# Diffusion one row tile ahead of the attention's products instead of three

## The chip, the cores and the metric

The kernel runs on one core of one Trainium2 chip. The metric is the device time of one execution in microseconds (us). A core has five engines that run beside each other: TensorE (PE in the profile, with its weight loads as PEld) multiplies matrices into PSUM, VectorE (DVE), ScalarE (ACT) and GpSimd (POOL) compute on tiles in SBUF and PSUM, and SyncE (SP) issues the DMA transfers. Each engine takes its instructions from a queue of its own, in order; where one engine needs the result of another, it waits on a semaphore.

## The reference

Four graph layers are applied to 3327 nodes with 256 features, each followed by a residual addition and a normalization over the features. The first three (neighbour mean, graph convolution with a Mamba block, graph attention) are not changed. Layer 3 is what matters here:

- `R = adj + I`, each row divided by its sum. Two steps are taken, n = 0 and 1, from `Xf = Xa = X`.
- In each step a top-p attention matrix `A` is made from `Xa`: `logits = q @ k.T`, a softmax over each row, then only the largest probabilities whose sum before them is below 0.9 are kept, and the row is divided by what is kept.
- The diffusion is `Xf = R @ Xf`, the attention `Xa = A @ Xa`, and `Z = Z + Xf @ U1[n].T + Xa @ U2[n].T`.
- The result is a layernorm of `X + Z` with gain and bias, then the residual and the last normalization.

## The kernel before

All arrays are float32. The nodes are padded to 26 row tiles of 128. A row tile of either matrix product, `R @ Xf` or `A @ Xa`, is a sum over 26 column tiles, that is 26 products of 128x128 by 128x256 on TensorE. The profile counts two matmul records for each such product.

Layer 3 runs as two passes over the row tiles, one for each step: pass 0 (the loop at L1163) and pass 1 (L1194). For a row tile a pass needs:

- the *scores* (`scores`, L803): q times k into PSUM (L817), copied by ACT into the row's `e` tile (L823 in pass 0; the copy made in program order, recorded as L801, in pass 1). One PSUM tile (`sc`, one buffer) is used for all of them.
- the *search* for the row's threshold. In pass 0 it is `search_short` (L916): maxima on DVE, one exponential over the row on ACT (L924), the thresholded row on DVE (L927). In pass 1 it is `search_long` (L933): two exponentials (L948, L950) and four counting passes (L963, L965, L995, L997) on ACT, and on DVE selections (L1015, L882, L1045) and at last the thresholded row (L1053). It is spread over three iterations of the loop by `yield`.
- the *diffusion* (`diffused`, L843, and `aggregated`, L829): GpSimd makes the row's own term `t` (L847, and in pass 1 with `s` loaded at L850 and added at L851), TensorE makes 26 products (L837) with adjacency blocks that SP loads in six transfers (L835, ring `at` of three buffers), and DVE writes the result `xf` (L856).
- the *attention's products* (`attended`, L859): groups of four 128x128 transposes of `e` (L866), copies out of PSUM on ACT (L868, or L801 in pass 1), and products (L870).
- the end of the row: in pass 0 `first` (L1063), which transposes `xf` and the attention's result (L1071) and multiplies them by the U matrices (L1078 to L1085); in pass 1 `second` (L1094), which reads `xf` at L1097, normalizes and stores.

How far the diffusion runs ahead is set by `DL`. In iteration i the rows to be diffused are

```
more = range(len(xfs), min(nt, i + DL + 1))
```

(L1167 and L1204), and `xf` has a ring of `DL + 2` buffers (L855). In pass 0 the first of these rows is emitted together with the scores of row i + 1 and any further ones after them; then follow the attention's products of row i. In pass 1, `slot` (L1207) deals out the diffusion's products between the steps of the scores, of the attention of row i - 1 and of the searches:

```
for _ in range(products * len(more)):
    next(spread, None)
```

The text of the program gives an order of work; the framework's scheduler then places the instructions on each engine's queue within the dependencies. Instructions passed through `here` or `in_order` keep the order of the text among themselves (in pass 1 the score products and copies, and ACT's six sweeps of the search); in pass 0 the score products have priority instead. Diffusion products have neither and are placed where the scheduler finds room for them.

With DL = 3, pass 0 diffuses rows 0, 1 and 2 in its first iteration (i = -1), then row i + 3 in iteration i, and nothing in the last three. Pass 1 begins at i = -2 with rows 0 and 1, then row 2 (i = -1), then row i + 3, and nothing from i = 23 on.

Of the kernel before, what the change touches and what calls it, by code (L numbers as in the profile page):

```python
# [35 lines left out]
UNDER = 24.0  # L36
HUGE = 1e38
J3 = 5
DL = 3
KC = 416  # L40


# [1 line left out]
def gnn_kernel(ctx: ExitStack, tc: tile.TileContext, n: int, a: dict, out: bass.AP):  # L44
# [546 lines left out]
    with tc.tile_pool(name="l3", bufs=1) as pool, tc.tile_pool(name="l3d", bufs=1, space=DRAM) as dram:  # L591
# [251 lines left out]
        def diffused(work, atp, psum, p, it, out, each=J3):  # L843

            rd = rdeg[:, it:it + 1]
            t = work.tile([P, D], F32, name="t")
            nc.gpsimd.tensor_scalar(t, (Y if p else X)[:, it, :], rd, None, op0=ALU.mult)  # L847
            if p:
                s = work.tile([P, D], F32, name="s")
                nc.sync.dma_start(s, sd[it])  # L850
                nc.gpsimd.tensor_tensor(t, t, s, op=ALU.add)  # L851
            for acc in aggregated(atp, psum, it, Y if p else X, each):
                if acc is None:
                    yield
            d = work.tile([P, D], F32, name="xf", bufs=DL + 2)  # L855
            nc.vector.scalar_tensor_tensor(d, acc, rd, t, op0=ALU.mult, op1=ALU.add)  # L856
            out.append(d)
# [291 lines left out]
        with tc.tile_pool(name="l3w", bufs=2) as work, tc.tile_pool(name="l3s", bufs=4) as sm, \  # L1149
# [3 lines left out]
            def start(p, t, es, searches, search):  # L1153
                q = work.tile([2 * DA, P], F32, name="q")
                nc.sync.dma_start(q, qd[p][t])
                es[t] = work.tile([P, npad], F32, name="e", bufs=4)
                searches[t] = search(work, sm, es[t], *(x[p][:, t:t + 1] for x in (tots, vs, kepts)),
                                     **({"halves": True} if p and t == nt - 1 else {}))
                return scores(work, psum, p, q, es[t])

            with tc.tile_pool(name="l3p", bufs=2, space=PSUM) as psum:
                es, searches, xfs, todo = {}, {}, [], None
                for i in range(-1, nt):  # L1163
                    parts = []
                    if i + 1 < nt:
                        parts.append(start(0, i + 1, es, searches, search_short))
                    more = range(len(xfs), min(nt, i + DL + 1))  # L1167
                    for j in more[:1]:
# [22 lines left out]
            with tc.tile_pool(name="l3q", bufs=3, space=PSUM) as psum:  # L1191
                es, searches, xfs = {}, {}, []
                result = iter(())
                for i in range(-2, nt + 1):  # L1194
# [7 lines left out]
                    if i + 2 < nt:  # L1202
                        logits = start(1, i + 2, es, searches, search_long)
                    more = range(len(xfs), min(nt, i + DL + 1))  # L1204
                    spread = (x for j in more for x in diffused(work, atp, psum, 1, j, xfs, 1))
# [188 lines left out]
```

## Time and profile before

| | |
|---|---|
| three timed runs, median | 3727.61 us |
| lowest and highest | 3721.43 and 3730.53 us |
| span of the profiled execution | 3731.3 us |
| busy PE, PEld | 3418.9 us (92%), 2538.2 us (68%) |
| busy DVE, ACT, POOL | 2581.8 us (69%), 1699.4 us (46%), 560.9 us (15%) |
| layer 3, pass 0: from its first score product to the last product of `first` | 1935.4 to 2851.8 us |
| layer 3, pass 1: from the first diffusion product to the end | 2852.5 to 3731.3 us |
| diffusion products, pass 0 and pass 1 | 307.9 and 348.0 us busy, 1352 records each |

How to read the profile: times count from the start of the span. A busy time is summed over instructions, so that overlapping ones count twice. A wait is the idle time of an engine ahead of an instruction, and it is put down to the instruction that released it. In a timeline each line is one instruction, or several alike in a row (xcount): start, duration, engine, line, operation, tile written <- tiles read, and in brackets the idle time before it and what ended it. The share of busy time is an average over the whole span; layer 3's two passes have different limits, so each is read by itself, in windows.

### The profile page before, as it was taken

The numbers are of one execution on the slowest core, as the hardware profiler recorded it, in microseconds if no ns is written. First come the engines' busy times: TensorE is split into PE (matmuls) and PEld (weight loads), VectorE is DVE, ScalarE is ACT, GpSimd is POOL, SyncE is SP. The second block draws the span as 40 slices with busy tenths as digits, with TensorE's granted clock in tenths as the row PEclk, the third lists the DMA queues.
The fourth block names the chain that finished last, engine by engine and source line by source line (L and its number), as shares of the span: only waits on it lengthen the run. The fifth ranks groups of instructions, "written<-read, shape, count | busy, mean of one in ns | idle before, by whom it ended". The sixth has DMA issues, their size and how long they took to land. (4 is left out here: it accounts for less than half of the span.)

```text
span 3731.3 us, 41342 instructions
## 1 busy us (share of the span) xinstructions
PE 3418.9 (92%) x14823; PEld 2538.2 (68%) x14823; DVE 2581.8 (69%) x5213; ACT 1699.4 (46%) x2716; POOL 560.9 (15%) x850
## 2 busy tenths in 40 slices
PE   9999998889888877699989999999999999999985
PEld 7888876555454433378867787787777677777764
DVE  1111588999999999877754444445451899999996
ACT  1000655644445564211122333333333888888883
POOL 0000012320211100011110000000000233333332
PEclk9999999989999888899989999999999999999998
DMA  7443343333333121144422221121112222222210
GB/s 243 138 139 98 104 110 97 94 82 94 88 89 88 51 56 47 39 154 145 145 92 86 61 61 53 57 64 51 56 46 62 78 57 65 66 66 66 65 39 7
DMA packets 151985, 307.87 MB, mean 83 GB/s; under 512 B 19858, under 2 KB 73266, under 8 KB 151634
## 3 DMA queue, kind: packets, MB, share of 16 engines
q1 hardware_dynamic: 151762, 305.06, 27.5%
q8 instruction: 120, 1.97, 0.2%
q14 instruction: 103, 0.84, 0.1%
HBM read 294.36 MB, written 10.65 MB: 82 GB/s over the span
## 5 line engine op out<-in xcount | busy, mean ns | idle before, releaser
L553 PE MATMUL y<-db,ident 128*128 128x512 f32 (+3 forms) x1024 | 439.9, 572 | 63.1 <-DVE db L547 63.1
L478 DVE TENSOR_TENSOR_SCAN db<-dA,db 128x2052 f32<-128x2052 f32 (+3 forms) x128 | 463.7, 3623 | 0.9
L553 PEld LDWEIGHTS y<-db,ident 128*128 128x128 f32 x1024 | 200.0, 210 | 255.5 <-issue 157.5
L870 PE MATMUL acc<-G,wt 128*128 128x256 f32 x1352 | 338.3, 394 | 18.3 <-ACT wt L801 17.8
L870 PE MATMUL acc<-X,wt 128*128 128x256 f32 x1352 | 343.6, 391 | 9.0 <-ACT wt L868 8.6
L837 PE MATMUL acc<-F,at 128*128 128x256 f32 x1352 | 348.0, 385 | 1.1 <-ACT q L611 0.6
L266 PE MATMUL cb<-F,at 128*128 128x256 f32 x1352 | 314.1, 386 | 2.0 <-ACT hn L287 2.0
L116 PE MATMUL acc<-xa,at 128*128 128x257 f32 x1352 | 308.3, 381 | 5.7 <-DMA at<-in_adjT 5.7
L870 PEld LDWEIGHTS acc<-X,wt 128*128 128x128 f32 x1352 | 242.5, 189 | 103.9 <-issue 41.3
L837 PE MATMUL acc<-X,at 128*128 128x256 f32 x1352 | 307.9, 381 | 0.6 <-DMA at<-in_adjT 0.6
L746 PE MATMUL acc<-F,at 128*128 128x257 f32 x1352 | 303.8, 381 | 0.8 <-ACT r L719 0.8
L870 PEld LDWEIGHTS acc<-G,wt 128*128 128x128 f32 x1352 | 250.9, 193 | 78.6 <-ACT wt L801 48.5
L266 PEld LDWEIGHTS cb<-F,at 128*128 128x128 f32 x1352 | 260.4, 194 | 60.9 <-issue 16.3
L882 DVE MAX8 cand<-e 128x8 f32<-128x128 f32 x676 | 142.2, 278 | 228.3 <-ACT e L823 216.8
L463 ACT ACTIVATE dA<-dt,A_log 128x512 f32<-128x512 f32 (+3 forms) x512 | 292.1, 633 | 4.1 <-DVE dt L420 3.9
L837 PEld LDWEIGHTS acc<-F,at 128*128 128x128 f32 x1352 | 238.5, 190 | 73.9 <-issue 46.6
L116 PEld LDWEIGHTS acc<-xa,at 128*128 128x128 f32 x1352 | 255.1, 190 | 42.9 <-issue 6.4
L837 PEld LDWEIGHTS acc<-X,at 128*128 128x128 f32 x1352 | 253.0, 191 | 41.1 <-issue 8.5
L746 PEld LDWEIGHTS acc<-F,at 128*128 128x128 f32 x1352 | 253.5, 190 | 36.5 <-issue 1.0
L470 DVE TENSOR_TENSOR db<-du,row 128x2052 f32<-128x2052 f32 (+3 forms) x128 | 240.9, 1882 | 47.7 <-PE y L553 37.9
L547 DVE TENSOR_TENSOR db<-db,row 128x2048 f32<-128x2048 f32 (+3 forms) x128 | 241.2, 1885 | 26.6 <-ACT carry L481 26.6
L868 ACT COPY wt<-tp 128x512 f32<-128x512 f32 (+1 forms) x182 | 93.5, 557 | 307.8 <-PE tp L866 307.6
(302 smaller groups left out, 5207.3 us busy)
## 6 DMA issues: line engine op xcount, KB each, us to landing
at<-in_adjT SPq DMA_DIRECT2D x102, 832.0 KB, 4.5
at<-in_adjT SPq DMA_DIRECT2D x260, 320.0 KB, 3.0
row<-bc SPq DMA_DIRECT2D x80, 512.0 KB, 4.8
at<-in_adjT SPq DMA_DIRECT2D x52, 576.0 KB, 4.5
at<-in_adjT SPq DMA_DIRECT2D x26, 512.0 KB, 3.6
row<-bc SPq DMA_DIRECT2D x16, 384.0 KB, 4.9
row<-bc SPq DMA_DIRECT2D x16, 256.0 KB, 5.3
xt<-in_xT SPq DMA_DIRECT2D x26, 128.0 KB, 4.1
```

The costliest lines, as they stand in the source:

```text
L116: nc.tensor.matmul(acc, at[:, j, :], rhs[:, j0 + j, :], start=(j0 + j == 0), stop=(j0 + j == nt - 1))
L266: nc.tensor.matmul(acc, at[:, j % JC, :], X0[:, j, :], start=(j == 0), stop=(j == nt - 1))
L463: nc.scalar.activation(dA[:, g, 1:], dt[:, g, :], AF.Exp, scale=A[:, g, s:s + 1])
L470: tc.keep_in_program_order(nc.vector.tensor_mul(by_group(dbs[(x[0] * DS + s) % 3], w), du, B[:, 0:1, :].to_broadcast([P, NG, 1 + w])))
L478: nc.vector.tensor_tensor_scan(h[:, :m], dAs[s % 2][:, :m], h[:, :m], initial=0.0, op0=ALU.mult, op1=ALU.add)
L547: nc.vector.tensor_mul(h, h, rows.pop(0)[:, 1:2, 1:].to_broadcast([P, NG, w]))
L553: nc.tensor.matmul(ys[g][:, :w], ident, h[:, g, :], start=False, stop=(s == DS - 1))
L746: nc.tensor.matmul(acc, at[:, j, :], F[:, j0 + j, :], start=(j0 + j == 0), stop=(j0 + j == nt - 1))
L837: nc.tensor.matmul(acc, at[:, j, :], rhs[:, j0 + j, :], start=(j0 + j == 0), stop=(j0 + j == nt - 1))
L868: copy(wt[:, :m, :], pt[:, :m, :])
L870: nc.tensor.matmul(acc, wt[:, j, :], rhs[:, j0 + j, :], start=(j0 + j == 0), stop=(j0 + j == nt - 1))
L882: nc.vector.max(cand[:, s * 8:(s + 1) * 8], z[:, s * SEG:(s + 1) * SEG])
```

## The change

One constant changes. Nothing else in the text does; the two expressions for `more` and the ring of `xf` follow from it.

```diff
@@ -36,7 +36,7 @@
 UNDER = 24.0
 HUGE = 1e38
 J3 = 5
-DL = 3
+DL = 1
 KC = 416
```

With DL = 1, pass 0 diffuses row 0 in iteration -1 and row i + 1 in iteration i, with nothing left for i = 25. Pass 1 diffuses nothing at i = -2, row 0 at i = -1, then row i + 1, and nothing at i = 25 and 26. Each pass still diffuses all 26 rows. The ring of `xf` has three buffers instead of five.

## The prediction

> **What bounds the kernel now.** The change touches layer 3 only, so I looked for where its two passes lie and what each waits for. First the table by stretches and the waits, then the timeline at the three places where the change moves work: the start of pass 0 (1929 us), the hand-over to pass 1 (2852 us), the end.
>
> Waits of pass 0 in its steady part (2040 to 2720 us): waiting engine and line, releaser, us in total, times, longest.
>
> ```profile
> ACT wt L868 <- PE tp L866: 234.9, 79, 9.3
> DVE cand L882 <- ACT e L823: 164.5, 59, 6.3
> ...
> DVE xf L856 <- PE acc L837: 71.5, 20, 3.6
> ...
> PE acc L870 <- ACT wt L868: 4.8, 20, 0.2
> ```
>
> ACT and DVE wait for TensorE; TensorE waits 4.8 us in 680. TensorE bounds pass 0. The row period, from one start of a row's transposes at L1071 to the next (2024.57, 2059.27), is 34.7 us.
>
> Pass 1, steady part: its stretch (busy us of PE, PEld, DVE, ACT, POOL, then clock, DMA), and the only waits of TensorE and of DVE there.
>
> ```profile
> 3111.00:3576.00 465.00, 456.83 (x2197) 338.96 (x2195) 445.32 (x1489) 390.10 (x379) 167.28 (x331) 1.00 0.22 66
> ```
>
> ```profile
> PE tp L866 <- DVE e L1053: 8.2, 15, 0.6
> ```
>
> ```profile
> DVE cs L902 <- DVE top L893: 0.5, 1, 0.5
> ```
>
> Here the bound is DVE: it waits once in 15 rows, while TensorE waits 0.55 us in each row for DVE's last step of a search (L1053). The period is 465/15 = 31.0 us. TensorE has only about half a microsecond to spare per row.
>
> Now the start of pass 1, ACT and TensorE (start us, duration, work, in brackets the idle time before it and what ended it):
>
> ```profile
> 2865.77 3.07 ACT L948 ACTIVATE junk<-e,neg 128x3328 bf16<-128x3328 f32 x1
> ...
> 2881.30 0.85 ACT L801 COPY e<-sc 128x832 f32<-128x832 f32 x1 [12.36 <-PE sc L817]
> 2882.05 3.07 ACT L950 ACTIVATE e<-e,neg 128x3328 f32<-128x3328 f32 x1
> ```
>
> ```profile
> 2868.84 11.52 PE L837 MATMUL acc<-F,at 128*128 128x256 f32 x52 [0.46 <-DMA at<-in_adjT]
> 2880.28 0.97 PE L817 MATMUL sc<-kT,q 64*128 64x416 f32 x4
> ...
> 2932.39 1.97 PE L866 MATMUL tp<-ident,e 128*128 128x128 f32 x8 [6.45 <-DVE e L1053]
> ```
>
> The 52 records are one row's diffusion (26 products, two records each). It stands ahead of the scores of row 1; ACT's copy of those scores stands ahead of the second exponential of row 0 (L950), which has its input long since. So row 0's search, and with it DVE, stands still for 12.36 us because of a diffusion that nobody needs yet. Later TensorE has done five diffusions and waits 6.45 us for that same search.
>
> The end, where the diffusions have run out:
>
> ```profile
> 3606.00:3668.00 62.00, 41.63 (x183) 29.68 (x181) 57.55 (x200) 48.80 (x47) 19.06 (x39) 0.92 0.02 5
> ```
>
> TensorE has 20 us of idle time in these two rows, DVE 4.5.
>
> **What the Trainium skill says.** "PSUM — Partial Sum Buffer", section "Engine vs sequencer instructions": ScalarE's and VectorE's queues are strict FIFO. The trace agrees: L950 sits behind the copy for 12.36 us. "Perfetto Trace Analysis", section "Optimization Strategy" (under performance opportunities): where the most contended engine changes over time, interleaving the regimes may help; here the start of pass 1 has a chain through ACT and DVE and the end has free TensorE time. "TensorE: Matmul & The Clock Gate", section "What's actually happening": after an idle window of about 3.4 us TensorE runs at half rate until it has been busy for about as long. The trace agrees: after 6.45 us idle, eight transposes took 1.97 us, against 1.04 at 2786.33.
>
> **The change, part by part.** DL only moves diffusions; their number stays 26 a pass. The program's order of instructions on each engine shows what moves, and that the rows between are ordered as before, row by row.
>
> *Pass 1, start.* Five diffusions stand ahead of the first attention product, three after the change; none is ahead of row 1's scores save most of the first. I follow the chain. The first two score pairs keep their times (2854.84, 2857.24). Then three products (0.43 us each) lie between pairs instead of four and six, so the fourth pair comes at 2862.04, its copy ends at 2863.97, and L948 runs 2864.1 to 2867.1 (1.7 us earlier). The next score pair is at 2864.44 on TensorE, so its copy follows L948 directly, at 2867.13 instead of 2881.30: 14.2 us earlier. From there every step (L950, copies, L963, L965, L948 of row 1, L995, L997) has the durations and order of before; TensorE's pairs, two to five products apart, arrive in time. L997 ends at 2890.2. DVE's part up to the end of L1053 (2906.74 to 2932.25, 25.5 us) carries one L856 less, 0.4 us (0.48 with overlap). The first attention product follows 14.6 us earlier, at 2917.8. DVE's steady work starts 14.6 us earlier too.
>
> The DMAs moved with it: the adjacency blocks of each diffusion (six loads on SP's queue, three ring slots), the s tile (L850) and two POOL steps (L847, L851). Behind them on SP wait the q loads (L1155). q of row 1 was issued at 2855.37, ahead of the moved blocks, and stays so; I get each block landing (3.0 us, row of 320 KB loads) within 1 us of its use, hidden under the ACT chain. L856 stands in DVE's queue between small steps of the search: its products end at 2870.8, 2885.5 and 2903.3, before DVE gets there, or while DVE waits for ACT anyway. At nothing.
>
> *Pass 1, middle and end.* Rows up to 21 have the order of before, and DVE bounds them: shift kept. Two more rows (23 and 24) carry a diffusion: 22.5 us of TensorE put into 20 us of idle time at the end, of which DVE sees only its L856, 2 x 0.4 us. In exchange DVE's 1.9 us wait at 3612.54 (attention products held behind a transpose that waits for L1053) sits in a row that becomes regular. Two regular rows, 62.0 us, against 61.5 us now (L1053 at 3606.31 and 3667.82): +0.5, at worst +1.5, at best -1.5. Sum of pass 1: -14.6 + 0.5 = -14.1.
>
> *Pass 0.* TensorE bounds it, so only its idle time counts. At the start the attention of row 0 now follows two diffusions directly. Its transposes are at 1975.3, but the copy out of PSUM is queued on ACT behind this:
>
> ```profile
> 1976.37 3.07 ACT L924 ACTIVATE e<-e,neg 128x3328 f32<-128x3328 f32 x1 [4.90 <-DVE neg L923]
> ```
>
> That ends at 1979.44, the copy takes 0.58, so TensorE idles from 1976.5 to 1980.1, 3.6 us. It comes back at half rate: after 2.3 us idle eight records took 3.65 instead of 1.89 us (3643.94), so +1.7. The two diffusions that covered this (11.30 us each, plus two waits of 0.32) leave: 23.2 - 5.3 = 17.9 us earlier. At the end two rows without a diffusion, 25.6 and 25.2 us (L1071 at 2752.2, 2777.79, 2802.99), become regular rows of 34.7: +18.6. So +0.7, with the half rate between nothing and 3 us and the wait between 2 and 4: -2.5 to +2.5. I take +1. A diffusion costs 9.3 us there and not 11.3, because eight of its products fill waits.
>
> *Ring of xf tiles.* Five buffers become three. A tile's last reader is in the row before its slot is written again, and in pass 1 on the same engine. No wait added; at nothing.
>
> Sum: -14.1 + 1 = -13.1 us against the profiled span of 3731.3. The three timed runs have a median of 3727.6 (3721.4 to 3730.5): 3714.5.
>
> **Rivals.** *Forecast*: as summed; 3708 to 3719 with the bounds above. Chance 0.70.
>
> *The gain is mostly lost*: pass 0's start costs 6 us or more (TensorE stays at half rate, or the copies on ACT also wait for L925), or the chain in pass 1 meets a late adjacency block. For it: several blocks land with less than 1 us to spare. Against: ACT's exponentials of 3.07 us each cover a microsecond. -14 + 7 = 3721; chance 0.20.
>
> *TensorE becomes the bound in pass 1* (slower side): place, the rows from 2918 us on. It idles 14.5 us there instead of 6.45, enters slow, and has 0.55 us to spare per row; two more diffusions lie ahead of it. The price: each microsecond by which a row exceeds 31 is paid in some 23 rows, so from 0.6 us per row (14.1/23) the gain is gone; at 1.2 us, 3727.6 - 13 + 28 = 3742. Against: the rows keep their order, and the clock stood at 1.00 there. Chance 0.05.
>
> *The transfer is hidden anyway*: DVE's start moves, but ACT and DVE then wait for the next row's scores and the end stays. For it: TensorE is 98% busy in pass 1. Against: the waits name DVE's L1053 in all 15 rows. 3728 to 3730; chance 0.05.
>
> That the scheduler puts the diffusions back is excluded by the order of instructions.
>
> **How the numbers follow.** Likeliest 3714.5. What a measurement tells from no change is 0.3%, 11 us, so the line lies at 3716.4, inside the forecast's own range: of its 0.70 I count 0.58 below that line; the second rival gives 0.06 more by half its spread; faster 0.64, same 0.30, slower 0.06. The range, 3707 to 3723, takes in the forecast and most of the second rival.
>
> **What would show it.** The gap of 12.36 us ahead of ACT's copy is gone; L1053 first starts near 2915 (shifted by what pass 0 does), with some 14 us of TensorE idle time before the first transposes there; period 31.0; at 1976 a TensorE wait of about 3.6 us for wt (L868); pass 1 begins within 3 us of 2852.5. Wrong, if row periods of pass 1 grow, or pass 0 ends over 3 us later.

## The result, and the profile after

| | kernel before | changed kernel |
|---|---|---|
| timed runs, median | 3729.07 us (4 runs, 3721.43 to 3733.05) | 3709.70 us (4 runs, 3707.88 to 3712.46) |
| ratio of the times | | 0.9951 (0.9934 to 0.9969) |
| span of the profiled execution | 3731.3 us | 3710.7 us |
| layer 3 begins (first score product, L817) | 1935.37 us | 1930.21 us |
| pass 0, from there to the first diffusion product on F | 917.11 us | 917.77 us |
| pass 1, from there to the end | 878.82 us | 862.72 us |

The kernel is faster by 0.5%. Pass 1 gives 16.1 us, pass 0 takes 0.7, and 5.2 us of the difference between the two profiles lie ahead of layer 3, where TensorE, VectorE, ScalarE and the transfers have the same order of instructions in both. (The ratios, here and in the experiments, are as recorded; they differ from the quotients of the medians by less than 0.0007.) The lines below are of the changed kernel and are read against those that the prediction shows of the kernel before.

ACT at the start of pass 1 (timeline: start, duration, work, idle time before it):

```profile
2859.55 3.07 ACT L948 ACTIVATE junk<-e,neg 128x3328 bf16<-128x3328 f32 x1
...
2862.61 0.83 ACT L801 COPY e<-sc 128x832 f32<-128x832 f32 x1
2863.35 3.07 ACT L950 ACTIVATE e<-e,neg 128x3328 f32<-128x3328 f32 x1
```

The copy that had waited 12.36 us for its scores now follows L948 with no idle time, and the second exponential, L950, comes right behind it. From the start of the pass to this copy it was 28.82 us (2881.30 - 2852.48); it is 14.63 (2862.61 - 2847.98). The part of these 14.2 us that is not the wait of 12.36 comes from the score products of row 0, between which TensorE now has fewer diffusion products.

TensorE at the same place, down to the first transposes of the attention:

```profile
2847.98 2.43 PE L837 MATMUL acc<-F,at 128*128 128x256 f32 x10 [0.63 <-ACT q L611]
...
2896.99 0.97 PE L817 MATMUL sc<-kT,q 64*128 64x416 f32 x4 [0.95 <-ACT e L801]
2897.89 1.13 PE L837 MATMUL acc<-F,at 128*128 128x256 f32 x4
2913.36 1.97 PE L866 MATMUL tp<-ident,e 128*128 128x128 f32 x8 [14.35 <-DVE e L1053]
```

TensorE now idles 14.35 us here, where it had idled 6.45, and the transposes still start 14.5 us earlier in the pass (65.38 us after its start instead of 79.91). More idle time on an engine, and a shorter program: the idle stretch is not what sets the end.

What releases these transposes is L1053, the last step of row 0's search on DVE. In the kernel before, with the first diffusion product of the pass, and then in the changed kernel:

```profile
2852.48 2.43 PE L837 MATMUL acc<-F,at 128*128 128x256 f32 x10 [0.63 <-ACT q L611]
...
2928.65 3.68 DVE L1053 SCALAR_TENSOR_TENSOR e<-e,v 128x3328 f32<-128x3328 f32 x1
```

```profile
2909.61 3.69 DVE L1053 SCALAR_TENSOR_TENSOR e<-e,v 128x3328 f32<-128x3328 f32 x1
```

From the start of the pass it was 76.17 us to this step and is 61.63 (2909.61 - 2847.98).

The steady part of pass 1, fifteen rows again: its stretch, then the waits of TensorE and DVE in it.

```profile
3093.00:3557.00 464.00, 455.46 (x2188) 337.78 (x2187) 444.41 (x1483) 389.03 (x374) 167.17 (x330) 1.00 0.22 67
```

```profile
PE tp L866 <- DVE e L1053: 8.5, 15, 0.9
...
DVE h L1097 <- PE tp L866: 0.3, 1, 0.3
```

Hardly anything has changed: 31 us a row, DVE waits once in fifteen rows, TensorE waits for DVE's L1053 in each. Over 21 rows, from L1053 of row 0 to that of row 21, the two kernels take 647.30 and 647.87 us.

The start of pass 0, TensorE and ACT:

```profile
1970.62 1.04 PE L866 MATMUL tp<-ident,e 128*128 128x128 f32 x8
1971.50 0.38 PE L1071 MATMUL pj<-ident,xf 128*128 128x128 f32 x2
1975.38 6.49 PE L870 MATMUL acc<-X,wt 128*128 128x256 f32 x16 [3.50 <-ACT wt L868]
...
1983.01 3.69 PE L870 MATMUL acc<-X,wt 128*128 128x256 f32 x16
```

```profile
1971.69 3.07 ACT L924 ACTIVATE e<-e,neg 128x3328 f32<-128x3328 f32 x1 [4.89 <-DVE neg L923]
...
1974.76 1.05 ACT L868 COPY wt<-tp 128x512 f32<-128x512 f32 x2
```

The price is there as foretold: TensorE waits 3.50 us for a copy that stands behind L924 on ACT, and its next 16 records take 6.49 us instead of 3.69.

The end. First the row stretch that answers to the one at 3606 us, then the last row, changed kernel and kernel before (of which the prediction showed only the stretch ahead of it):

```profile
3600.00:3662.00 62.00, 56.12 (x276) 45.52 (x275) 59.64 (x200) 42.01 (x41) 19.96 (x41) 0.97 0.13 39
```

```profile
3678.12 1.28 PE L866 MATMUL tp<-ident,e 128*128 128x128 f32 x10 [2.61 <-DVE e L1047]
3679.48 3.72 PE L870 MATMUL acc<-G,wt 128*128 128x256 f32 x16
...
3693.33 0.21 PE L1137 MATMUL acc<-f,ones 128*1 128x26 f32 x2
```

```profile
3696.18 1.94 PE L866 MATMUL tp<-ident,e 128*128 128x128 f32 x8 [5.61 <-DVE e L1047]
3698.00 5.69 PE L870 MATMUL acc<-G,wt 128*128 128x256 f32 x16
...
3714.04 0.21 PE L1137 MATMUL acc<-f,ones 128*1 128x26 f32 x2
```

The diffusions that left the start fill TensorE's idle time near the end, 41.63 us busy of 62 before and 56.12 after. A by-product is in the last row. After 2.61 us of idle time its transposes and products run at full rate (16 records in 3.72 us); after 5.61 us the first eight transposes had taken 1.94 us, against 1.04 for eight at full rate, and the next 16 records 5.69. The clock granted to TensorE was 0.83 from 3696.1 to 3714 us in the kernel before; it is 1.00 from 3678 to 3693 us in the changed one. From the first transposes to the last product it took 17.9 us and takes 15.2.

### The profile page after: what moved, and what is told of

The parts are those of the page before. It is cut to its first block, busy times and chain, and to the rows that moved or that the text cites. A ratio compares the mean times of both kernels' runs of the same rounds, so it can differ in the third digit from the quotient of the medians.

```text
span 3710.7 us, 41335 instructions
## 1 busy us (share of the span) xinstructions
PE 3409.8 (92%) x14823; PEld 2534.8 (68%) x14823; DVE 2583.6 (70%) x5213; ACT 1700.1 (46%) x2716; POOL 557.6 (15%) x850
## 3 DMA queue, kind: packets, MB, share of 16 engines
q8 instruction: 120, 1.97, 0.2%
```

## The experiments

The theory: the gain is the start of pass 1 alone. A diffusion that nobody needs yet stood ahead of row 1's scores on TensorE's queue, ACT's copy of them stood ahead of row 0's second exponential, and so DVE, which bounds the pass, began 14.5 us late; pass 0 is neutral. Rivals: that both passes share the gain; that what counts is the number of diffusions moved to the end, into idle time; that TensorE, with more diffusions left for the attention's rows, becomes the bound. For the first four experiments and the sixth the constant is split, so that each pass has a depth of its own (shown against the kernel before):

```diff
-DL = 3
+DL0, DL1 = 3, 1
@@ ring of xf, L855
-            d = work.tile([P, D], F32, name="xf", bufs=DL + 2)
+            d = work.tile([P, D], F32, name="xf", bufs=5)
@@ pass 0, L1167
-                    more = range(len(xfs), min(nt, i + DL + 1))
+                    more = range(len(xfs), min(nt, i + DL0 + 1))
@@ pass 1, L1204
-                    more = range(len(xfs), min(nt, i + DL + 1))
+                    more = range(len(xfs), min(nt, i + DL1 + 1))
```

### Pass 1 alone

The diff above as it stands.

> Only pass 1 runs one row ahead (DL 1), pass 0 keeps three, the xf ring keeps five buffers. Chain theory (row 0's search no longer stands behind a diffusion): from the first diffusion product of pass 1 to the end some 16 us less than before (878.8 us before, 862.7 in the changed kernel), the wait of 12.36 us ahead of ACT's copy gone, and pass 0 as before (917.1 us from its first score product to the first diffusion product of pass 1). Rival, that the gain of about 19 us lies in pass 0 or ahead of layer 3: less than 10 us less in total.

Measured: 3714.35 us against 3729.38, ratio 0.9966 (0.9952 to 0.9981). In its profile pass 1 takes 863.12 us against 862.72 in the changed kernel, and L1053 of row 0 starts 61.62 us after the pass begins against 61.63. Pass 1's part of the change, alone, gives 15.7 us inside pass 1. In total it is 15.0 us, so the rival, under 10, falls. The whole change gave 19.4 and, in a second measurement (below), 19.0; where the other 4 us lie is not settled by these runs.

### Pass 0 alone

```diff
-DL0, DL1 = 3, 1
+DL0, DL1 = 1, 3
```

> Only pass 0 runs one row ahead, pass 1 keeps three, ring of five. Theory: pass 0 loses about 5 us at its start (wait for ACT's copy, half rate) and gets 4 to 5 back at its end, so the total is the same as before within 2 us, and pass 1 lasts 878.8 us as before, with the wait of 12.36 us in it. Rival, that the 5 us by which the changed kernel was ahead at the start of layer 3 come from the change itself: the first score product of layer 3 near 1930 us and a total 4 to 6 us below before.

Measured: 3730.15 us against 3729.38, ratio 1.0001 (0.9993 to 1.001). That pass 0 shares the gain falls, and so does the rival that its part of the change brings the earlier start of layer 3: that is at 1935.36 us here. Pass 1 takes 879.1 us, with the wait of 12.36 us in it. TensorE's wait at its start is the same, the half rate a little shorter:

```profile
1979.56 5.41 PE L870 MATMUL acc<-X,wt 128*128 128x256 f32 x16 [3.50 <-ACT wt L868]
```

### Two ahead in pass 1, and none

```diff
-DL0, DL1 = 3, 1
+DL0, DL1 = 3, 2
```

```diff
-DL0, DL1 = 3, 1
+DL0, DL1 = 3, 0
```

> Pass 0 as before, pass 1 two rows ahead: one diffusion instead of two stands ahead of row 1's scores, and one moves to the end. Chain theory: 12 products (5.2 us) remain ahead of row 1's scores after row 0's, of which 1.7 us hide behind ACT's first exponential; the first L1053 comes 11 to 13 us earlier relative to the start of pass 1, three quarters of the gain, and pass 1 takes 864 to 868 us. Rival (what counts is how many diffusions fill TensorE's idle time at the end): half the gain, pass 1 near 871 us.

> Pass 0 as before, pass 1 diffuses a row in the same iteration as its search ends (DL 0), so that one diffusion more goes from the start to the end and TensorE idles some 25 us ahead of the first attention products. Chain theory: the chain through ACT and DVE is already free of diffusions at one row ahead, so L1053 first ends within 1 us of there and pass 1 takes 861 to 865 us, like the changed kernel. Rival (filling of the end counts): another 8 us less, near 855 us. Rival (TensorE becomes the bound after a long idle time): row periods above 31.0 us, pass 1 over 870 us.

Measured, with the kernel before and the first experiment for comparison:

| ahead in pass 1 | timed | ratio to before | pass 1 in the profile | L1053 of row 0, from the pass's start |
|---|---|---|---|---|
| 3 (before) | 3729.38 us | 1 | 878.82 us | 76.17 us |
| 2 | 3717.34 us | 0.9967 (0.9956 to 0.9979) | 865.45 us | 64.22 us |
| 1 | 3714.35 us | 0.9966 (0.9952 to 0.9981) | 863.12 us | 61.62 us |
| 0 | 3712.73 us | 0.9960 (0.9946 to 0.9974) | 862.21 us | 61.41 us |

One diffusion less makes nearly the whole gain, the second some 2 us, the third under one. The last step is not clear of scatter: each line but the first has one profile, six profiles with one row ahead in pass 1 lie between 862.1 and 863.1 us, and the intervals of the three ratios overlap. Both expectations of the chain theory, 864 to 868 and 861 to 865 us, held. A gain by the number of diffusions moved to the end would be in even steps. Pass 1's length follows the start of L1053 instead: from there to the end it is 800.8 to 801.5 us in the three experiments and 802.7 before. With none ahead TensorE idles 25.3 us ahead of the first transposes, more diffusions than in the change lie beside the attention and yet the row period stays 31 us: TensorE does not become the bound.

### The place, not the number

The third test of that keeps what is ahead and moves only where it stands: three ahead as before in the steady part, but nothing diffused in the first iteration of pass 1, whose diffusions stand ahead of row 1's scores.

```diff
-                    more = range(len(xfs), min(nt, i + DL + 1))
+                    more = range(len(xfs), min(nt, i + DL + 1) if i > -2 else 0)
```

> DL stays 3 in both passes; the only edit is that pass 1 emits no diffusion in its first iteration, so that none but the filled-in products of row 0 stand ahead of row 1's scores. Nearly five diffusions still lie ahead of the attention's products of row 0 (124 of 130 products). Theory (the place ahead of row 1's scores is what costs): the wait of 12.36 us is gone and the first L1053 comes 14 to 15 us earlier relative to the start of pass 1 (near 61.7 instead of 76.2); as diffusions 1 and 2 now stand ahead of row 2's scores, row 1's search is late by some 6 us, and 8 to 12 us of the gain reach the end (pass 1 near 867 to 871 us). Rival (the number of diffusions that leave the start for the end counts): nearly nothing left the start, so L1053 and the end stay within 2 us of before (pass 1 near 878 us).

Measured: 3719.52 us against 3731.95, ratio 0.9966 (0.9955 to 0.9977). In the order of instructions 120 of the 130 diffusion products ahead of the attention's first transposes still stand there (78 in the change), and pass 1 takes 867.13 us, 11.7 less than before: the place decides. But L1053 of row 0, expected near 61.7 us from the start of the pass, came at 66.23. This part of the expectation missed, since the diffusions of rows 1 and 2 now stand ahead of the next row's scores, and the same knot comes again one row later (ACT):

```profile
2889.33 0.19 ACT L997 ACTIVATION_READ_ACCUMULATOR junk<-e,c 128x1 f32 x1
2896.54 0.85 ACT L801 COPY e<-sc 128x832 f32<-128x832 f32 x1 [7.03 <-PE sc L817]
2897.29 3.07 ACT L950 ACTIVATE e<-e,neg 128x3328 f32<-128x3328 f32 x1
```

The copy holds L950 of row 1 by 7.03 us. Row 1 has time (its L1053 comes 28.8 us after row 0's), but on DVE its steps stand in the midst of row 0's chain:

```profile
2900.49 0.16 DVE L956 TENSOR_TENSOR c<-c,tot 128x1 f32<-128x1 f32 x1 [2.46 <-ACT e L950]
...
2900.95 1.94 DVE L1015 SCALAR_TENSOR_TENSOR z<-e,c 128x1664 f32<-128x1664 f32 x1
```

So L1053 of row 0 comes 4.6 us later than in the change, and pass 1 is 4.4 longer. The two numbers agree. Against the kernel before L1053 is 9.9 us earlier; most of the rest of the 11.7 is a shorter stretch from L1053 of row 21 to that of row 24, 90.08 us instead of 91.87.

### Two ahead in pass 0, one in pass 1

If the 3.50 us wait at the start of pass 0 is a real cost, one more diffusion behind the first transposes should cover it.

```diff
-DL0, DL1 = 3, 1
+DL0, DL1 = 2, 1
```

> Pass 0 two rows ahead, pass 1 one row ahead, ring of five. In pass 0 one diffusion now stands between row 0's first transposes and its products and covers the wait of 3.5 us for ACT's copy, which the changed kernel has at 1971 us; one row at the end still gets a diffusion whose fillers save 1.8 us. Theory: pass 0 some 2 us shorter than before (near 914 us from its first score product to the first diffusion product of pass 1, against 917.1 and 917.8), pass 1 near 862.7: some 3 us below the changed kernel in total, hardly more than the measurement tells. Rival (the wait is filled by work that has to be done anyway and only moves): equal to the changed kernel within 1 us.

In the profile the diffusion lies in the gap, and the products behind it run at full rate:

```profile
1975.44 0.38 PE L866 MATMUL tp<-ident,e 128*128 128x128 f32 x2
1976.02 11.56 PE L837 MATMUL acc<-X,at 128*128 128x256 f32 x52 [0.20 <-DVE f L1060]
...
1988.48 3.72 PE L870 MATMUL acc<-X,wt 128*128 128x256 f32 x16
```

Pass 0 takes 913.23 us, the shortest of all profiles, but the timed median is 3713.13 us (ratio 0.9945, 0.9932 to 0.9959) beside 3712.97 for the changed kernel on the same chip (next part). Some 3 us less were expected, and the profile shows 2 to 4.5 us less in pass 0; the timed runs do not show it, and agree with the rival. A version that beats the changed kernel is not shown.

### The changed kernel again, and the time ahead of layer 3

The changed kernel was run three times more, the kernel before once more, and once the changed kernel with five buffers in the ring of `xf`, to see whether the smaller ring moves anything:

```diff
-            d = work.tile([P, D], F32, name="xf", bufs=DL + 2)
+            d = work.tile([P, D], F32, name="xf", bufs=5)
```

> The changed kernel once more, on the same chip as the others. Layer 3 takes about 1780 us as in its first profile (1795.9 before), so 15 to 16 us less in total; if the 5 us by which it was ahead at the start of layer 3 are scatter between executions, its start of layer 3 lies anywhere from 1930 to 1936 us and the ratio nearer 0.996 than 0.995.

> The kernel before, once more. It is there for the point at which layer 3 begins (first score product of L817), 1935.4 us in the first profile of this kernel and between 1930.2 and 1936.3 in the others, with the same instruction order ahead of it. If those six microseconds are scatter between executions, this profile may lie anywhere in that range. If they belong to the program, it should come within a microsecond of 1935.4. Layer 3 itself should take 1795.9 within 1.

> The change, with the ring of the diffusion operands kept at five tiles instead of three. If the smaller ring (which moves other tiles to other addresses) is what makes layer 3 begin near 1930 in both profiles of the changed kernel, this one should begin at 1933 to 1936, and layer 3 should take 1777 to 1780 as in the change. If the ring is of no account, the start is no different from the changed kernel's beyond the scatter.

> The changed kernel a third time, for the point at which layer 3 begins: 1930.2 and 1930.7 in its two profiles so far. A third value within a microsecond of these speaks for something in the program; one of 1933 or more for scatter between executions. Layer 3 itself 1777 to 1781.

The second run of the changed kernel was timed: 3712.97 us against 3731.95, ratio 0.9952 (0.9938 to 0.9966). The gain of 19.0 us is more than the 15 to 16 expected. The other three have a single time each: before 3729.64 (and 3727.52 in one more run beside them), changed with five buffers 3710.61, changed 3709.70 us. From the profiles:

| profile | layer 3 begins | pass 0 | pass 1 |
|---|---|---|---|
| before, first and second | 1935.37, 1932.56 | 917.11, 916.56 | 878.82, 878.68 |
| changed, first to third | 1930.21, 1930.74, 1930.32 | 917.77, 915.36, 915.37 | 862.72, 862.10, 862.21 |
| changed, five buffers | 1930.69 | 915.56 | 862.55 |
| the other six experiments | 1932.24 to 1936.26 | 913.23 to 916.91 | |

The smaller ring shows no effect. Layer 3 takes 1795.9 and 1795.2 us in the kernel before, 1780.5, 1777.5 and 1777.6 in the changed one. Two executions of the kernel before begin it at times 2.8 us apart, so a good part of the 5.2 us is scatter. Most of it arises far ahead of layer 3: one load of an earlier layer (L265) is issued at 547.19 us in the first profile of the kernel before, at 544.48 in the second, and at 543.88 to 544.64 in the four of the changed kernel and its five-buffer form. The twelve profiles fall into two groups there, 543.9 to 544.7 and 546.9 to 547.9 us, and the third and fourth experiments, three deep in pass 0, are in the earlier one. Yet the four profiles with a depth of one in both passes are the four earliest of twelve, within 0.5 us. TensorE's wait there is put down to a transfer, in all four and in the kernel before alike, and is no shorter in them as a rule (8.34 to 10.03 us, before 8.97 and 9.93):

```profile
1930.21 1.76 PE L817 MATMUL sc<-kT,q 64*128 64x416 f32 x4 [8.34 <-DMA at<-in_adjT]
```

GpSimd's last four instructions ahead of this point stand in another order with one row ahead in pass 0, but so they do in the second experiment, which begins layer 3 at 1935.36 us. Why the four come 2 us earlier than the second profile of before, no run settles.

## Why the prediction was right, and where its sum was off

It foretold 13.1 us of gain and 3714.5 us; against the profile of before the gain is 20.6 us, of which 15.4 are in layer 3 (17.2 between the means of four and of two profiles), and the median is 3709.70, 4.8 us below the forecast and inside its range. The mechanism held; three sizes did not.

- *Pass 1, start: -14.6.* Measured -14.54 (L1053 of row 0 at 61.63 instead of 76.17 us from the pass's start). The 14.2 us by which ACT's copy was to come earlier are 14.19. The adjacency blocks and DVE's L856, put at nothing, cost nothing that shows: TensorE's one wait for a block there is 0.36 us. L1053 begins at 2909.61 us and not near 2915; 4.5 us of the difference are the earlier start of the pass. The idle time before the transposes is 14.35 us against 14.5 worked out.
- *Pass 1, middle: no change.* Held: 647.3 and 647.9 us for 21 rows, against the rival in which TensorE becomes the bound, whose own threshold was 0.6 us a row.
- *Pass 1, end: +0.5.* This is the term that was mis-sized. The sum compared rows 23 and 24 and stopped at DVE's last L1053; the last row was left out as unchanged. Rows 23 and 24 took 60.1 us, against 61.5 before and 62.0 worked out; but DVE's L1097, which stood ahead of the last L1053, now comes behind it, together with an L856, so most of this comes back before L1047. From L1053 of row 21 to that of row 24 it is 91.08 instead of 91.87 us, from there to L1047 27.47 instead of 26.26, and from L1047 to the last product 17.30 instead of 19.96. Sum with the 0.6 of the middle and 0.1 in the final step: -1.6 us. In the last row TensorE's products are themselves the path, so the rate at which they run goes straight into the time; TensorE is busy for 17.67 of the 17.90 us from 3696.1 us in the kernel before, at the clock of 0.83. The prediction showed a granted clock of 0.92 for the rows just ahead and did not ask what it would be in this one. The other profiles bear this out: this stretch takes 19.7 to 20.1 us in all five with two or three rows ahead in pass 1, and 17.3 to 17.4 in six of the seven with one or none; in the seventh, the first experiment, it takes 19.0, and a slow stretch follows its wait (last section).
- *Pass 0: +1.* Measured +0.66 in the first pair of profiles, -0.4 between the means of the five with one row ahead in pass 0 and the six with three (916.0 and 916.3). That the first pair comes so near is partly luck. The start gave 16.6 us where 17.9 was worked out (to L1071 of row 1), and the end took 18.9, not 18.6; this is made good by the last row, from its L1071 to pass 1, where eight products of the kernel before ran at half rate (L1078, 3.65 us): 18.25 us instead of 19.90. Of the six profiles with three ahead four have 19.8 to 19.9 there and two 18.25, so this is not the change's doing. Within the start, the wait worked out as 3.6 us is 3.50; the half rate, taken as +1.7, is +2.8 in the first profile (6.49 - 3.69) and +1.7 in the four others with this start (5.41). The bounds given, -2.5 to +2.5, hold all of them.
- *Ahead of layer 3: not in the sum.* It is 5.2 us of the 20.6, partly scatter, in part open. "Pass 1 begins within 3 us of 2852.5" missed for this reason (2847.98), not by pass 0.
- *Rivals.* That the gain is mostly lost to pass 0 is excluded by the second experiment, and a late adjacency block by the 0.36 us. That the move is hidden anyway falls with the lengths of pass 1.

On the Trainium skill: what "PSUM — Partial Sum Buffer", section "Engine vs sequencer instructions", says of strict FIFO queues carried the result on both engines, ACT's 12.36 us and, in the fifth experiment, DVE's 2.46. The window of about 3.4 us in "TensorE: Matmul & The Clock Gate", section "What's actually happening", which the prediction used elsewhere, could have pointed to the last row: 5.61 us of idle time lie above it and 2.61 below, and the measured rates go the same way. It is no sharp limit for a single wait, though: in the stretch of short waits that the prediction cites, a wait of 2.30 us was followed by twelve transposes at full rate (1.50 us) and then by the eight records at half rate. The same section says that the window runs freely and that the number of slow products varies from run to run, which agrees with the spread in the last section here.

## What to carry to other kernels

Before work is put ahead as filler, look at what stands behind it on the same queue. If that is the input of another engine's in-order queue, what the other engine's work does not hide of the filler goes into the chain (here 12.36 us of the 15.6 between two pairs of scores, 2864.65 to 2880.28), even where the filler's engine has idle time a little later. Ask of an idle stretch what ends it, and whether that chain passes through the filler; here 14 us of idle TensorE in front of the attention cost less than the work that would have filled them. And follow the sum to the last instruction: in the final row no other work lies beside the path, and a wait there can also set the rate of what follows it.

## What was not expected of the hardware

The half rate after a wait is not a fixed charge. After the same wait of 3.50 us the same 16 records took 6.49 us in one profile and 5.41 in four others, against 3.69 at full rate. In the last row it began late: with three ahead in pass 0 and one in pass 1, a wait of 3.91 us was followed by transposes at full rate (10 in 1.28 us) and then by products at a slower one:

```profile
3678.33 1.28 PE L866 MATMUL tp<-ident,e 128*128 128x128 f32 x10 [3.91 <-DVE e L1047]
3679.69 5.41 PE L870 MATMUL acc<-G,wt 128*128 128x256 f32 x16
```

A gap of 14.35 us cost hardly more than one of 6.45: the first eight transposes took 1.97 us after both, and the eight products behind them 3.78 and 3.58; in the first experiment, after 14.34 us, these took 2.97.
